# Filling two half-arrays by a count of time: the beats of a fused PixArt block

## The chip, the core and the metric

The kernel runs on one core of a Trainium2 chip. The metric is device time in microseconds (us) of one execution of the whole program; smaller is better. Beside the times of the runs there is one profiled execution, taken by the hardware profiler, from which all rows in this document come. Engines are named as in the profile: PE is TensorE's matmuls, PEld its weight loads, DVE is VectorE, ACT is ScalarE, POOL is GpSimd, SP is SyncE, which issues most DMAs.

## The reference

One transformer block with 16 batch rows of 256 tokens, 256 features, 16 heads of 16. Layout changes left out:

```python
shift_a, scale_a, gate_a, shift_m, scale_m, gate_m = jnp.split(silu(c) @ W_mod + b_mod, 6, axis=-1)
x_norm = modulate(_ln(x), shift_a, scale_a)
q, k, v = jnp.split(x_norm @ W_qkv + b_qkv, 3, axis=-1)
attn_w = softmax(einsum('bhqd,bhkd->bhqk', q, k) * scale)
x = x + gate_a[:, None] * (einsum('bhqk,bhkd->bhqd', attn_w, v) @ W_proj + b_proj)
q_c = _ln(x) @ W_qc + b_qc
k_c, v_c = jnp.split(_ln(context) @ W_kvc + b_kvc, 2, axis=-1)
c_attn_w = softmax(einsum('bhqd,bhsd->bhqs', q_c, k_c) * scale)
x = x + einsum('bhqs,bhsd->bhqd', c_attn_w, v_c) @ W_cproj + b_cproj
h = gelu(modulate(_ln(x), shift_m, scale_m) @ W_mlp1 + b_mlp1)
x = x + gate_m[:, None] * (h @ W_mlp2 + b_mlp2)
```

So each batch row has a self-attention, then a cross-attention over 256 context tokens, then a feed-forward part.

## The kernel before

The work of one attention of one batch row is a *unit*. There are 32: self-attentions of rows 0 to 3 first (units 0 to 3), then alternately a self-attention and, four rows behind, a cross-attention (`seq`, line 748); from unit 4 to 27 an even number is a self-attention (tiles named `_s`) and an odd one a cross-attention (`_c`). The last four units are cross-attentions, and the feed-forward part of all rows follows.

The main loop has one *step* for each unit, of eight *beats* (`beat(n, k)`, line 1025). Every engine's instructions keep the order in which the program writes them, so the order within `beat` is the order of every queue; only semaphores between engines and the filling of queues are left to the machine.

Each beat starts with `visit` (line 1006): four score matmuls `s` of the next unit, whose row maxima VectorE takes (`mx`, one reduction over both banks of the tile `s`), and four transposed score matmuls `st` of the present unit, of which ScalarE takes the exponential (`pt`). There is one `s` tile and one `st` tile of two banks each, so the next beat's `s` waits for this beat's maximum, and the next beat's `st` for this beat's exponential. Beats 0 and 4 then multiply the probabilities with V (`o`, 32 matmuls, emptied by ScalarE as `oT`). The other beats hold *lane work*.

Lane work uses one half of the array's rows at a time: partitions 0 to 63 are one row tile (lane 0), partitions 64 to 127 the other (lane 1), and instructions for both can be in flight together. A projection (K, Q, V or the output projection P) with its three products of split numbers is 12 matmuls of 64 rows by 256 columns on each half, `lane(o, half)` at line 418: first eight of the high parts, then four of the low part. Lane 0 opens the PSUM bank and lane 1 adds to it, some beats later; a `PE.nop()` that waits (`after`, line 314) stands ahead of the second half. Transposes too come in halves (`half_turns`, line 320): four instructions a half for a tile of 256 by 256, one a half for the maxima. `beside(a, b)` (line 454) takes one instruction from lane 0's list and one from lane 1's in turn; `take(it, n)` (line 449) is n instructions of a projection that goes on later.

In step n the lane work is, with u+2 and u+3 the units two and three ahead: beat 1, Q of u+2 beside P of u-2 and the second half of this unit's maxima; beats 2 and 3, transposes T of the normalised input of u+3 and A of the attention output of u-1, V of u+2 in lane 0, Q of u+2 in lane 1; beat 5, maxima of the next unit (`psm`, sent on as `m`), transposes aT of u-1's normalised output, K of u+3 in lane 0, V of u+2 in lane 1; beat 6, transposes T[1] (the cross-attention's query side, when u+3 is one: `lx`, which holds in even steps) and A of this unit, K of u+3 in lane 1; beat 7, P of u-1 in lane 0.

A transposed tile goes from PSUM through ScalarE (`evac`, tile `y`) to GpSimd, which splits it (`cut`, tiles `xTh` and `xTl`). `keep` (line 528) is ScalarE's copy of V out of PSUM. PSUM beside `s` and `st` has two rings of two banks: LONG for projections, SHORT for transposes, maxima and `o`; a bank is free when its last reader is done. In odd steps from 5 to 23 beat 6 is `light` (line 1054): its `s` goes to one bank of the tile and one of the SHORT ring, with a reduction for each.

Of the kernel before, what the change touches and what calls it, by code (L numbers as in the profile page):

```python
# [3 lines left out]

# [17 lines left out]
def pixart_block(  # L22
# [45 lines left out]
    def ps_gen(name, tag=None):  # L68


        if tag is None and ps_turn[0] is not None:
            ps_turn[0] ^= 1
            tag = (SHORT, LONG)[ps_turn[0]]
        tag = tag or SHORT
        return psum.tile([P, 512], F32, tag=tag, name=name, bufs=2)
# [234 lines left out]
    def whole(pieces, o):  # L310
        for i, p in enumerate(pieces):
            PE.transpose(o.ps[:, i * P:(i + 1) * P], p, ident)

    def after(name):

        gate = PE.nop()
        tc.add_manual_dep(gate.ins, name, mybir.DependencyInfo(
            mybir.DependencyClass.Sync, mybir.DependencyReason.DATA), reason="one bank, two halves of the array")

    def half_turns(pieces, o):  # L320


        done = []

        def half(h):
            rows = slice(64 * h, 64 * h + 64)
            for i, p in enumerate(pieces):
                if i == 0 and done:
                    after(done[0])
                ins = PE.transpose(o.ps[:, i * P + 64 * h:i * P + 64 * h + 64], p[rows], ident[rows, rows])  # L330
                if i == len(pieces) - 1:
                    done.append(ins.ins.name)
                yield
        return half(0), half(1)

    def transposed(src, name, scale=None, pool=False):
# [81 lines left out]
    def lane(o, half):  # L418


        rows = slice(half * 64, half * 64 + 64)
        if half:
            after(o.seen)
        for low in (False, True):
            for f in range(2):
                for k in range(KC):
                    for a, b in (((1, 0),) if low else ((0, 0), (0, 1))):
                        xT, W = o.src.xT, o.W
                        x_, w_ = xT[a][rows, k], W[b][rows, k]
                        if o.tok:  # L430
                            x_ = x_[:, f * P:(f + 1) * P]
                        else:
                            w_ = w_[:, f * P:(f + 1) * P]
                        ins = PE.matmul(o.ps[:, f * N:(f + 1) * N], *((x_, w_) if o.tok else (w_, x_)),
                                        start=o.fresh, stop=(half == 1 and low and k == KC - 1),
                                        skip_group_check=True)
                        o.seen = ins.ins.name
                        o.fresh = False
                        yield

    def lane0(x):
        if x:
            x.ps, x.fresh = ps_gen(f"ps_{x.name}", LONG), True
        return lane(x, 0) if x else iter(())

    def lane1(y):
        return lane(y, 1) if y else iter(())

    def take(it, n):
        for _ in range(n):  # L450
            next(it, None)
            yield

    def beside(a, b):
        for _ in zip_longest(chain(*a), chain(*b)):
            pass

    def to_stack(W, src, bias, dst, which, name):

# [301 lines left out]
    nu = len(units)  # L761
# [258 lines left out]
        later.append(lambda: exp(units[n], k, bank))  # L1020

    none = (), ()
    rest_x = rest_y = ()

    def beat(n, k):
        nonlocal rest_x, rest_y
        if n < 0:
            visit(n, k, (st, sp)[k % 2])
            return
        cur, prev, nxt = unit(n), unit(n - 1), unit(n + 1)  # L1030
        q2, q3, q4 = (v if v and v.n >= m else None
                      for v, m in zip(map(unit, (n + 2, n + 3, n + 4)), (1, 2, 3)))
        p1, p2, p3 = (v and v.post for v in map(unit, (n - 1, n - 2, n - 3)))
        apart = n > nu - 4
        if n - 2 > nu - 5:
            p2 = None
        if n - 3 > nu - 5 or p3 and p3.hurry:
            p3 = None
        lc = q4 if q4 and q4.kind == "c" else None
        ls = q4 if q4 and q4.kind == "s" else None  # L1040
        lx = q3 if q3 and q3.kind == "c" else None
        late = lx and lx.b in (0, 1, B - 2, B - 1)
        early = lc if lc and lc.b not in (0, 1, B - 2, B - 1) else None
        if k == 0 and q2:
            q2.K.high()
            q2.K.send_high()
        if k == 2 and p2:
            p2.end()
        if k == 4 and q2:
            q2.Q.high()  # L1050
            q2.Q.send_high()
        if k == 6 and q2:
            q2.V.keep()
        light = k == 6 and nxt and 3 < n < nu - 4 and not lx
        home = sp
        if light:
            home = sp[:, 0], ps_gen("s1", SHORT)
        elif nxt and n * 8 + k >= nu * 8 - 17 and k % 2:
            home = ps_gen("s0", LONG), ps_gen("s1", LONG)
        visit(n, k, home)  # L1060
        exps()
        if k == 0:
            if prev:
                av_part(prev, 2)
                av_part(prev, 3)
            if q2:
                q2.K.low()
                q2.K.send_low()
            if p3:
                p3.add()  # L1070
            if ls and n > 0:
                load(ls)
            if lc:
                lc.ln[0].steps[0]()
            if p1:
                p1.gate()
        elif k == 1:
            m = m_halves(cur, 1) if cur else none
            x, y = lane0(q2 and q2.Q), lane1(p2)
            beside([m[0], x], [take(y, 4), m[1], y])  # L1080
            if cur:
                m_send(cur, 1)
            if lc:
                lc.ln[0].steps[1]()
                lc.ln[0].steps[2]()
        elif k == 2:
            T = q3.T[0].halves() if q3 else none
            A = p1.halves(1) if prev else none
            x, y = lane0(q2 and q2.V), lane1(q2 and q2.Q)
            beside([T[0], A[0], take(x, 2)], [take(y, 10)])  # L1090
            rest_x, rest_y = [x], [T[1], A[1], y]
            if p2 and p2.hurry:
                p2.add()
        elif k == 3:
            beside(rest_x, rest_y)
            if q3:
                q3.T[0].evac()
                q3.T[0].cut()
            if prev:
                p1.norm(1)  # L1100
        elif k == 4:
            if cur:
                av_part(cur, 0)
                av_part(cur, 1)
            if q2:
                q2.Q.low()
                q2.Q.send_low()
            if p3:
                p3.store()
            if late:  # L1110
                for f in lx.ln[1].steps:
                    f()
            if ls and not late:
                ls.ln[0].steps[0]()
                ls.ln[0].steps[1](False)
        elif k == 5:
            m = m_halves(nxt, 0) if nxt else none
            aT = p1.aT.halves() if prev else none
            x, y = lane0(q3 and q3.K), lane1(q2 and q2.V)
            beside([m[0], take(x, 7), aT[0], x], [take(y, 2), aT[1], m[1], y])  # L1120
            if nxt:
                m_send(nxt, 0)
            if prev:
                p1.aT.evac()
                p1.aT.cut()
            if ls and late:
                for f in ls.ln[0].steps:
                    f()
            elif ls:
                ls.ln[0].pow()  # L1130
                ls.ln[0].steps[2]()
            if early:
                early.ln[1].steps[0]()
            v = unit(n + 5)
            if v and v.kind == "c":
                load(v)
        elif k == 6:
            if cur:
                cur.post.begin()
            T = lx.T[1].halves() if lx else none  # L1140
            A = cur.post.halves(0) if cur else none
            y = lane1(q3 and q3.K)
            beside([T[0], A[0]], [take(y, 8 if lx else 4)])
            rest_y = [T[1], A[1], y]
            if early:
                early.ln[1].steps[1]()
                early.ln[1].steps[2]()
            if prev and apart:
                p1.proj(0)
                p1.proj(1)  # L1150
        elif k == 7:
            beside([lane0(None if apart else p1)], rest_y)
            if lx:
                lx.T[1].evac()
                lx.T[1].cut()
            if prev and apart:
                p1.end()
                p1.add()
                p1.store()
            if cur:  # L1160
                cur.post.norm(0)
# [97 lines left out]
```

## Time and profile before

| | |
|---|---|
| median of 3 runs (lowest to highest) | 798.84 us (797.94 to 800.02) |
| the profiled execution's own time | 799.69 us |
| its span, first to last instruction | 797.9 us |
| mean granted TensorE clock | 0.999 |
| busy: PE / DVE / ACT / POOL | 97% / 74% / 70% / 66% |
| TensorE matmul instructions | 10066 |
| bytes moved by DMA | 87.96 MB, mean 110 GB/s |

The span is what the engines' instructions cover; the execution's own time is 1.8 us longer. Most instructions are issued through one helper, so their line is L51 and groups are told apart by the tiles they write and read. In a row of the timeline the columns are start, duration, engine, line, operation, output<-input, shape and count; in brackets stands the idle time before it and what ended it. In a row of stretches the columns are the stretch, its length, the busy time of PE, PEld, DVE, ACT and POOL with counts, the granted clock, the DMA share and GB/s. The chain of waits is followed back from the last instruction of a stretch; its rows give start, duration and what was worked on. In a row of a group the numbers behind the bar are busy us, mean ns of one, and idle us before them.

### The profile page before, as it was taken

How to read it: one execution, taken by the hardware profiler on the slowest of the kernel's cores; microseconds unless marked ns; L12 is line 12 of the kernel's file. 1: busy time of each engine (PE TensorE's matmuls, PEld its weight loads, DVE VectorE, ACT ScalarE, POOL GpSimd, SP SyncE). 2: the span in 40 equal slices, each digit the busy share in tenths (PEclk: the TensorE clock that was granted, in tenths of full speed). 3: DMA queues.
4: the chain of work that ended last, by engine and by line, in shares of the span. 5: the costliest groups of instructions: out<-in, count | busy, mean ns of one | idle time of the engine just before them, and what ended most of it. 6: DMA issues, size and time to landing. Idle time of an engine off the chain costs nothing.

```text
span 797.9 us, 25010 instructions
## 1 busy us (share of the span) xinstructions
PE 771.4 (97%) x10066; PEld 668.6 (84%) x10066; DVE 589.5 (74%) x1037; ACT 557.1 (70%) x961; POOL 529.4 (66%) x497
## 2 busy tenths in 40 slices
PE   8999999999999999999999999999899999999997
PEld 8778777888887887888888888877679999999997
DVE  5877878787788788888888888876674656656662
ACT  4267777787787877877777778776556666666663
POOL 6757849595775859567495878774546656666653
PEclk9999999999999999999999999999999999999999
DMA  6654444435344544534444554534311321211312
GB/s 206 146 152 130 109 120 123 109 107 154 104 133 108 148 122 108 161 97 128 122 127 141 138 146 121 159 100 120 95 43 42 93 61 60 81 59 62 81 41 53
DMA packets 89942, 87.96 MB, mean 110 GB/s; under 512 B 9506, under 2 KB 85572, under 8 KB 89828
## 3 DMA queue, kind: packets, MB, share of 16 engines
q1 hardware_dynamic: 89364, 85.58, 38.6%
q8 instruction: 80, 1.31, 0.7%
q0 software_dynamic: 192, 0.52, 0.3%
q14 instruction: 34, 0.28, 0.1%
q10 hardware_dynamic: 272, 0.26, 0.1%
HBM read 26.97 MB, written 8.46 MB: 44 GB/s over the span
## 4 chain that ended last, share of the span: by engine, by line
PE 60%; DVE 15%; POOL 9%; ACT 8%; issue 4%; DMA 2%; SPq 1%; POOLq 0%; ACTq 0%
PE o L51 14%; PE s L51 10%; PE st L51 7%; DVE mx L51 6%; DVE xn_m L51 4%; PE ps_qc L51 3%; PE ps_q L51 3%; POOL hl L51 3%; PE ps_v_c L51 3%; PE ps_P_s L51 3%; PE ph L51 3%; PE ps_k L51 2%; PE ps_v_s L51 2%; PE ps_kc L51 2%; PE ps_P_c L51 2%
## 5 line engine op out<-in xcount | busy, mean ns | idle before, releaser
L51 DVE TENSOR_REDUCE mx<-s 128x4 f32<-128x1024 f32 (+1 forms) x267 | 308.9, 1162 | 99.5 <-PE s L51 95.5
L51 ACT ACTIVATE pt<-st 128x1024 f32<-128x1024 f32 x252 | 259.5, 1030 | 79.8 <-PE st L51 68.2
L51 PE MATMUL s<-big 63*128 63x256 f32 (+1 forms) x1024 | 132.7, 315 | 4.1 <-DVE mx L51 1.8
L51 POOL TENSOR_TENSOR hl<-hf,hh 128x512 fp32r<-128x512 f32 x64 | 89.1, 1402 | 54.4 <-ACT hh L51 54.2
L51 PE MATMUL o<-pt,v 128*32 128x256 f32 x2048 | 123.8, 382 | 1.3 <-DVE A_c L51 0.4
L51 PEld LDWEIGHTS s<-big 63*128 63x128 f32 (+1 forms) x1024 | 86.5, 185 | 44.6 <-DVE mx L51 10.7
L51 PE MATMUL st<-big 64*128 64x256 f32 (+1 forms) x1024 | 116.2, 285 | 6.7 <-ACT pt L51 4.1
L51 PEld LDWEIGHTS st<-big 64*128 64x128 f32 (+1 forms) x1024 | 89.0, 186 | 12.2 <-ACT pt L51 6.7
L51 PEld LDWEIGHTS o<-pt,v 128*32 128x32 f32 x2048 | 60.4, 109 | 43.4 <-ACT y_s L51 3.1
L51 ACT ACTIVATE hf<-ph,bT 128x256 f32<-128x256 f32 x120 | 50.4, 474 | 27.5 <-PE ph L51 27.4
L51 ACT ACTIVATE hh<-ph,bT 128x256 fp32r<-128x256 f32 x120 | 50.5, 473 | 22.7 <-PE s L51 8.3
L51 ACT COPY oT<-o 128x512 f32<-128x512 f32 x63 | 37.0, 587 | 36.9 <-PE o L51 36.9
L51 PE MATMUL ph<-wqch,wself 128*128 128x256 f32 x256 | 51.4, 284 | 0.0
L51 PE MATMUL ph<-wkch,wself 128*128 128x256 f32 x256 | 51.4, 285 | 0.0
L51 POOL CAST xTh_c<-y_c 128x512 fp32r<-128x512 f32 x16 | 10.0, 626 | 56.5 <-ACT y_c L51 51.0
L51 PE MATMUL s<-big,hh 128*128 128x256 f32 x256 | 46.7, 281 | 0.0
L51 PE MATMUL st<-big,hh 128*128 128x256 f32 x256 | 46.5, 281 | 0.0
L51 DVE TENSOR_SCALAR xn_m<-x,mv_m,rs_m 128x256 f32<-128x256 f32 x32 | 38.2, 1234 | 10.8 <-POOL rs_m L51 10.8
L51 PEld LDWEIGHTS ph<-wqch,wself 128*128 128x128 f32 x256 | 41.5, 189 | 0.4 <-issue 0.4
L51 PEld LDWEIGHTS ph<-wkch,wself 128*128 128x128 f32 x256 | 41.5, 189 | 0.2
L51 PE MATMUL ps_k<-xTh_s,wself 64*128 64x256 f32 (+1 forms) x232 | 41.5, 293 | 0.0
L51 PE MATMUL ps_v_s<-wself,xTh_s 64*128 64x256 f32 x224 | 41.5, 295 | 0.0
(226 smaller groups left out, 2513.1 us busy)
## 6 DMA issues: line engine op xcount, KB each, us to landing
big<-h_kc SPq DMA_DIRECT2D x64, 128.0 KB
big<-h_qc SPq DMA_DIRECT2D x64, 128.0 KB
big<-h_k SPq DMA_DIRECT2D x62, 128.0 KB
big<-h_q SPq DMA_DIRECT2D x62, 128.0 KB
big<-l_k SPq DMA_DIRECT2D x32, 128.0 KB
big<-l_q SPq DMA_DIRECT2D x32, 128.0 KB
c<-in_ctx_dram SPq DMA_DIRECT2D x16, 256.0 KB
g<-gd SPq DMA_DIRECT2D x16, 256.0 KB
```

Source lines behind the costliest of these rows:

```text
L51: i = f(*a, **k)
```

## The change

Four edits, all in the order of lane work:

1. `beside` no longer takes turns. Each instruction yields its length, 1 for a projection matmul and `HALF = 0.53` for a half transpose, and the next instruction comes from the lane whose sum is smaller.
2. Lane work is spread differently over beats 2, 3, 5, 6 and 7. T and A are done within beat 2, the one half of A ahead of the other and opposite T; V takes 5 matmuls of lane 0 there and 7 in beat 3. Beat 5 holds 7 of K's and 7 of V's 12 matmuls and their last 5 move to beat 6, with the transposes of that beat in both lanes; K's second half is all in beat 7 beside P.
3. What hangs on these: T's `evac` and `cut` come at the end of beat 2 and no longer of beat 3; V's `keep` at the end of beat 6 and no longer at its start; `m_send` behind aT's `evac` and `cut`.
4. The `light` beat is gone: `s` of beat 6 always uses its own tile.

```diff
+    HALF = 0.53
...
@@ half_turns
-                yield
+                yield HALF
@@ lane
-                        yield
+                        yield 1
...
     def take(it, n):
         for _ in range(n):
-            next(it, None)
-            yield
+            yield next(it, 1)
 
     def beside(a, b):
-        for _ in zip_longest(chain(*a), chain(*b)):
-            pass
+        ab, at = [chain(*a), chain(*b)], [0, 0]
+        while min(at) < 1e9:
+            i = at[1] < at[0]
+            at[i] += next(ab[i], 1e9)
...
@@ beat
-        if k == 6 and q2:
-            q2.V.keep()
-        light = k == 6 and nxt and 3 < n < nu - 4 and not lx
         home = sp
-        if light:
-            home = sp[:, 0], ps_gen("s1", SHORT)
...
@@ k == 2
-            beside([T[0], A[0], take(x, 2)], [take(y, 10)])
-            rest_x, rest_y = [x], [T[1], A[1], y]
+            beside([T[0], take(x, 5), A[0]], [A[1], take(y, 5), T[1]])
+            rest_x, rest_y = x, y
+            if q3:
+                q3.T[0].evac()
+                q3.T[0].cut()
@@ k == 3
-            beside(rest_x, rest_y)
-            if q3:
-                q3.T[0].evac()
-                q3.T[0].cut()
             if prev:
                 p1.norm(1)
+            beside([rest_x], [rest_y])
@@ k == 5
-            beside([m[0], take(x, 7), aT[0], x], [take(y, 2), aT[1], m[1], y])
-            if nxt:
-                m_send(nxt, 0)
+            beside([m[0], take(x, 4), aT[0], take(x, 3)], [aT[1], take(y, 1), m[1], take(y, 6)])
+            rest_x, rest_y = x, y
             if prev:
                 p1.aT.evac()
                 p1.aT.cut()
+            if nxt:
+                m_send(nxt, 0)
@@ k == 6
-            y = lane1(q3 and q3.K)
-            beside([T[0], A[0]], [take(y, 8 if lx else 4)])
-            rest_y = [T[1], A[1], y]
+            beside([A[0], take(rest_x, 5), T[0]], [T[1], take(rest_y, 5), A[1]])
+            if q2:
+                q2.V.keep()
@@ k == 7
-            beside([lane0(None if apart else p1)], rest_y)
+            beside([lane0(None if apart else p1)], [lane1(q3 and q3.K)])
```

More of the change, by code (lines that the diff above doesn't have):

```diff
@@ L1 @@
 from collections import defaultdict
-from itertools import chain, zip_longest
+from itertools import chain
 from contextlib import ExitStack
@@ L1022, in pixart_block @@
     none = (), ()
-    rest_x = rest_y = ()
+    rest_x = rest_y = iter(())
     def beat(n, k):
@@ L1051, in beat @@
             q2.Q.send_high()
-        if k == 6 and q2:
-            q2.V.keep()
-        light = k == 6 and nxt and 3 < n < nu - 4 and not lx
         home = sp
-        if light:
-            home = sp[:, 0], ps_gen("s1", SHORT)
-        elif nxt and n * 8 + k >= nu * 8 - 17 and k % 2:
+        if nxt and n * 8 + k >= nu * 8 - 17 and k % 2:
             home = ps_gen("s0", LONG), ps_gen("s1", LONG)
```

## The prediction

> **What bounds the kernel now.** I read the page first, for the busiest engine, then one stretch of 100 us from the middle, then the timeline of a single step of the loop beat by beat, engine by engine, and last the chain of waits for the beats that are longer than their work.
>
> ```profile
> PE 771.4 (97%) x10066; PEld 668.6 (84%) x10066; DVE 589.5 (74%) x1037; ACT 557.1 (70%) x961; POOL 529.4 (66%) x497
> ```
>
> ```profile
> 300.00:400.00 100.00, 98.77 (x1540) 82.53 (x1531) 82.62 (x141) 78.83 (x122) 68.25 (x67) 1.00 0.46 124
> ```
>
> TensorE counts as busy 98.8% of a middle stretch at the full granted clock (1.00), but a busy TensorE may have one half of its array empty, and the mean hides which beats it limits. The start of each beat's `s` matmuls shows the beats. Step 15 (current unit a cross-attention, "odd") runs from 298.78 to 315.80; step 16 ("even") follows.
>
> ```profile
> 298.78 0.48 PE L51 MATMUL s<-big 63*128 63x256 f32 x4
> 301.29 0.50 PE L51 MATMUL s<-big 63*128 63x256 f32 x4
> 303.39 0.43 PE L51 MATMUL s<-big 63*128 63x256 f32 x4
> 305.14 0.50 PE L51 MATMUL s<-big 63*128 63x256 f32 x4
> 306.96 0.50 PE L51 MATMUL s<-big 63*128 63x256 f32 x4
> 309.65 0.51 PE L51 MATMUL s<-big 63*128 63x256 f32 x4
> 312.10 0.28 PE L51 MATMUL s<-big 63*128 63x256 f32 x1
> ...
> 313.40 0.51 PE L51 MATMUL s<-big 63*128 63x256 f32 x4
> 315.80 0.47 PE L51 MATMUL s<-big 63*128 63x256 f32 x4
> ...
> 323.96 0.51 PE L51 MATMUL s<-big 63*128 63x256 f32 x4
> 326.49 0.50 PE L51 MATMUL s<-big 63*128 63x256 f32 x4
> 328.94 0.28 PE L51 MATMUL s<-big 63*128 63x256 f32 x1
> ...
> 330.89 0.50 PE L51 MATMUL s<-big 63*128 63x256 f32 x4
> 332.82 0.47 PE L51 MATMUL s<-big 63*128 63x256 f32 x4
> ```
>
> Differences give beats 0 to 7 of the odd step: 2.51, 2.10, 1.75, 1.82, 2.69, 2.45, 1.30, 2.40 (17.02 us). Of the even step, beats 4 to 7: 2.53, 2.45, 1.95, 1.93.
>
> Inside a beat the halves work at their own rates:
>
> ```profile
> 303.87 0.22 PE L51 MATMUL psT_s<-ident,xn_s 64*128 64x64 f32 x1
> 303.90 0.28 PE L51 MATMUL ps_qc<-xTh_q,wqch 64*128 64x256 f32 x1
> ...
> 304.30 0.23 PE L51 MATMUL psA_s<-ident,oT 64*128 64x64 f32 x1
> 304.37 0.28 PE L51 MATMUL ps_qc<-xTh_q,wqch 64*128 64x256 f32 x1
> ```
>
> The first and last of eight transposes start 0.43 apart, 0.061 each; the first and fifth projection matmul start 0.47 apart, 0.117 each (one "slot"). In the program's order the eighth transpose stands behind the seventh of these matmuls, yet it starts before the fifth. So TensorE's queue already lets the quicker half run ahead: a beat costs about the longer half's own time, not the count of pairs.
>
> Beats that end before TensorE's work would allow are held by VectorE, whose maximum must be out of the `s` banks before the next beat's `s`:
>
> ```profile
> 303.86 1.22 DVE L51 TENSOR_REDUCE mx<-s 128x4 f32<-128x1024 f32 x1
> ...
> 305.68 1.22 DVE L51 TENSOR_REDUCE mx<-s 128x4 f32<-128x1024 f32 x1 [0.60 <-PE s L51]
> ```
>
> ```profile
> 326.43 0.74 DVE L51 BATCH_NORM_STATS2 st_s<-x 128x6 f32<-128x256 f32 x2
> 327.09 0.30 DVE L51 BATCH_NORM_AGGREGATE mv_s<-st_s 128x2 f32<-128x6 f32 x2
> ...
> 327.50 1.22 DVE L51 TENSOR_REDUCE mx<-s 128x4 f32<-128x1024 f32 x1
> 329.61 1.22 DVE L51 TENSOR_REDUCE mx<-s 128x4 f32<-128x1024 f32 x1 [0.89 <-PE s L51]
> ```
>
> Beat 2: the maximum starts 0.47 after `s`, ends at 305.08, and `s` follows at 305.14. Beat 3: 0.54, ends 306.90, `s` at 306.96. Even beat 6: 0.67 (a half still had backlog), ends 330.83, `s` at 330.89. So there is a floor: 1.75, 1.82 and 1.95 for the three.
>
> **The change part by part.**
>
> *Filling by time, beats 2 and 3.* Lane work of beat 2 was the longer half's 10 slots, now 4 + 4 transposes at 0.53 and 5 slots, 9.24; beat 3 falls from 10 slots to 7. Both sit on the floor of 1.75 and 1.82, so I put the gain at zero; bounds: 0 and -0.08 (beat 3 at beat 2's floor).
>
> *Beat 5.* Before: 0.53 + 7 + 2.12 + 5 = 14.65 slots a half. Now 0.53 + 4 + 2.12 + 3 = 9.65. The five slots go to beat 6: 5 x 0.117 = 0.58, so 2.45 becomes 1.87. In the odd step VectorE permits it (0.54 + 1.22 + 0.06 = 1.82, as in beat 3). In the even step it doesn't: its beat 4 also holds LayerNorm statistics, its maximum starts only 1.01 after `s` (327.50 against 326.49) and ends at 328.72; with 0.06 the next `s` is at +2.29. So the even beat 5 gains only 2.45 - 2.29 = 0.16.
>
> *Beat 4, odd.* The transposed tile is now evacuated at the end of beat 2, ahead of the beat-3 exponential on ScalarE. The chain shows what the old place cost:
>
> ```profile
> 306.92 0.82 ACT y_s L51 x2
> 307.74 0.04 issue
> 307.79 1.93 PE o L51 x32
> ```
>
> `o` takes the bank that `y_s` empties and waited for it. The even step, with one 0.58 evacuation, shows the beat without that wait: 2.53. Gain 2.69 - 2.53 = 0.16. The evacuation now goes ahead of exponential 3: it ends some 0.1 + 0.82 after beat 2's lane work (1.63, below), at 2.55, and that exponential could not start before 1.75 + 0.85 = 2.60 anyhow (0.85 is beat 5's, next fence). Its cut stands in POOL's queue behind the same work as before.
>
> *Beats 6 and 7, and V one step on.* ScalarE's order changes:
>
> ```profile
> 310.50 1.03 ACT L51 ACTIVATE pt<-st 128x1024 f32<-128x1024 f32 x1
> 311.42 0.25 ACT L51 ACTIVATE m<-psm 16x128 fp32r<-16x128 f32 x1
> 311.87 0.59 ACT L51 COPY y_as<-psT_as 128x512 f32<-128x512 f32 x1 [0.20 <-PE psT_as L51]
> 312.53 0.59 ACT L51 COPY v<-ps_v_c 128x512 f32<-128x512 f32 x1
> 313.01 1.03 ACT L51 ACTIVATE pt<-st 128x1024 f32<-128x1024 f32 x1
> ```
>
> Now: exponential 5, `y`, `m`, exponential 6, `v`, exponential 7. Counted from beat 5's `s`: exponential at 0.85 (310.50 - 309.65), `y` 0.92 later at 1.77, `m` at 2.25 (0.48 after a copy, as 312.53 to 313.01), done 2.50. In beat 6 the first transposes need the banks of `y` (2.36) and, being the second bank in the ring, of `m` (2.50); in the odd step TensorE comes there at 1.87 + 0.48 = 2.35 (0.48 as in beat 2) and waits 0.15, with everything behind it in its one queue. Lane work of odd beat 6 is 7.12 slots, 0.83, done by 3.4: the floor is later. Maximum 6 starts when the statistics let it (1.76 + 0.66, the step from 326.43 to 327.09, is 2.42; `s` + 0.54 is 2.41), ends 3.64, and `s` 7 is at 3.70. Exponential 6 starts at 1.87 + 0.85 = 2.72, `v` 0.92 later, done 4.23; the output projection, which takes V's bank, comes there at 3.70 + 0.48 to 0.61 (beats 2 and 5): at most 0.05 of wait. Beat 7 has 12 slots as the even one has, 1.93. So odd beats 6 and 7: 1.83 + 1.93 = 3.76, against 3.70 with the split maximum that is dropped: a loss of 0.06. Even: `s` 6 at 2.29 comes after `m`; the maximum 0.54 later ends 4.05, `s` 7 at 4.11, beat 6 is 1.82 and not 1.95, because both halves of beat 5 now end together: gain 0.13; beat 7 unchanged.
>
> *Queues moved past.* `m` goes behind `y` on ScalarE; its two DMAs follow on SP:
>
> ```profile
> 312.06 1.43 SPq L51 DMA_DIRECT2D big<-m  x2
> ```
>
> They are issued by 2.41 + 1.43 = 3.84 after beat 5's `s`, now 2.50 + 1.43 = 3.93, and first read 0.3 into the next step, at 5.95 instead of 6.45: 2.0 us of slack for landing instead of 2.6. POOL's cut could become the next late thing:
>
> ```profile
> 295.32 0.61 POOL L51 CAST xTh_ac<-y_ac 128x512 fp32r<-128x512 f32 x1 [2.76 <-PE ps_v_s L51]
> ...
> 309.49 0.61 POOL L51 CAST xTh_s<-y_s 128x512 fp32r<-128x512 f32 x1
> ```
>
> ```profile
> 310.26 0.36 PE L51 MATMUL ps_k<-xTh_s,wself 64*128 64x256 f32 x1
> ```
>
> From the first cut of an even step POOL works without a gap to 310.10, 14.78 us; K in odd beat 5 needs that. The cut will start at 2.42 in even beat 5, so it ends at 17.20; K wants it at 16.7 + 0.61 = 17.3. Slack 0.1; without it K waits at most some 0.3 us in each odd step.
>
> *The price that no row has.* Transpose against transpose, one in each half, does not occur before; now it does, eight pairs in beat 2 and eight in an even beat 6. Lower bound 0.061 a pair (each half at its own rate). Upper, far: two weight loads in a row, 0.28:
>
> ```profile
> L51 PEld LDWEIGHTS psT_s<-ident,xn_s 64*128 64x128 f32 (+1 forms) x116 | 10.9, 139 | 1.0 <-POOL xn_s L51 0.9
> ```
>
> Eight transposes and four matmuls with their loads start in 303.87 to 304.30, 0.036 an instruction, hence 0.072 a pair; this is nearest in kind and I take it. Beat 2 is then 0.47 + 8 x 0.072 + 0.58 = 1.63, under the floor.
>
> *Sum.* Ten odd steps (5 to 23): -0.58 - 0.16 + 0.06 = -0.68 each, -6.8. Eleven even steps (6 to 26): -0.16 - 0.13 = -0.29, -3.2. Steps 1 and 3 have no split maximum: -0.74 each, -1.5; step 25 likewise without the beat-4 part, -0.6. Steps 0, 2, 4 and from 27 on I leave at zero, some because their beat 6 waits for a late normalisation that comes no sooner. Together -12.1. The profiled execution of 799.69 becomes 787.6 (its span 797.9 becomes 785.8); it stands 0.85 above the median of the runs shown, 798.84, so the forecast on that scale is 786.7.
>
> **Rivals.** *Slower: transposes in both halves get in each other's way.* Place: beat 2 of some 27 steps and beat 6 of eleven. The cost over the floors is 27 x (8p - 0.69) + 11 x (8p - 0.77) = 304p - 27; it eats the 12.1 us at p = 0.128 a pair, about one after the other (2 x 0.061 = 0.122). At the 0.139 of one full load a pair it is +15.2, and the time 802. For it: loads are long (139 ns) and never seen side by side as a pair; against it: 0.036 an instruction above. The Trainium skill's page "TensorE: Matmul & The Clock Gate", section "LDWEIGHTS (loading the stationary operand)", gives a load as its columns over 1.2 ns, 107 ns for 128; were the two loads strictly one after the other, a pair would take an estimated 213 ns and the time come out near 824. By that rule, three loads per 0.117 us in beat 2 would not fit; the trace has them.
>
> *The gain is mostly given back to the floors.* If the maximum starts 0.67 after `s` as in even beat 6, and not 0.5, beats 2, 3, 5 and 6 rise by 0.1 to 0.2, together some 0.35 a step over 24 steps, 8.4 us: 795. For it: VectorE and ScalarE are at 83% and 79% of a middle stretch already. The skill's "TensorEngine Tiling (Array Packing)", section "PSUM Bottleneck", says the same in general: tiling speeds up TensorE and not the emptying of its banks. The trace agrees, with the floor of 1.75 to 1.95 under 1.22 us of maximum.
>
> *More than forecast.* Beats 3 and 6 fall to 1.75 as well, 2 x 0.08 over 24 steps, -3.8: 783.
>
> *The count of time does nothing,* since the queue runs ahead anyhow: true of beats 2 and 3, and in the sum as zero; beat 5 is different, since work leaves it.
>
> **How the numbers follow.** Forecast 786.7: chance 0.57, by itself 783.5 to 791 (POOL's 0.3 in ten steps, the bounds of beat 3). Floors, 795 (791 to 799): 0.20. More, 783 (780 to 784): 0.10. Slower, 802 and up: 0.13. A measurement here tells 0.3%, 2.4 us. Faster takes the forecast, the third and two thirds of the second: 0.80; same 0.07; slower 0.13. The range leaves out the slower case and the tails: 780 to 798.
>
> **What will show it.** Odd beat 5 at 1.9 and even beat 5 at 2.3; odd beat 6 at 1.85, with a single maximum, odd beat 7 at 1.9; odd beat 4 at 2.53 with no `y_s` ahead of `o`; beats 2 and 3 unchanged. Steps of 16.4 (odd) and 16.7 (even). Wrong if beat 2 grows past 1.8 (pairs), if TensorE waits for `v`, `m` or POOL's `xTh_s` by more than 0.3, or if maxima start later than 0.55 after `s`.

## The result and the profile after

The changed kernel takes 801.57 us (median of 20 runs, 798.84 to 806.3), the kernel before 799.15 (20 runs beside them, 797.47 to 800.04): ratio 1.0034, 95% interval 1.0020 to 1.0049. It is slower by a third of a per cent where 1.5% faster was forecast. Its profiled execution took 800.28 us with a span of 798.2, one of its quicker ones. Of all runs told below one is left out of medians and ratios, the first of g4_mix: it took 894.72 us at a mean granted clock of 0.753.

The busy line of the page of the changed kernel, and the middle stretch in the columns of the one shown before (PE, PEld, DVE, ACT, POOL, clock, DMA share, GB/s):

```profile
PE 766.0 (96%) x10066; PEld 656.9 (82%) x10066; DVE 589.3 (74%) x1027; ACT 562.0 (70%) x961; POOL 528.4 (66%) x497
```

```profile
300.00:400.00 100.00, 98.13 (x1558) 80.89 (x1552) 83.93 (x139) 80.39 (x123) 69.28 (x69) 1.00 0.45 125
```

Ten reductions fewer (1027 against 1037: the light beats), and in the middle 1558 matmuls in 100 us, not 1540: there the kernel is 1.2% quicker. The `s` rows of the timeline of the changed kernel, the end of step 14, step 15 (odd) and step 16 (even):

```profile
298.68 0.42 PE L51 MATMUL s<-big 63*128 63x256 f32 x4
301.13 0.50 PE L51 MATMUL s<-big 63*128 63x256 f32 x4
303.24 0.43 PE L51 MATMUL s<-big 63*128 63x256 f32 x4
305.01 0.48 PE L51 MATMUL s<-big 63*128 63x256 f32 x4
306.82 0.50 PE L51 MATMUL s<-big 63*128 63x256 f32 x4 [0.25 <-DVE mx L51]
309.41 0.50 PE L51 MATMUL s<-big 63*128 63x256 f32 x4
311.53 0.41 PE L51 MATMUL s<-big 63*128 63x256 f32 x4
313.27 0.50 PE L51 MATMUL s<-big 63*128 63x256 f32 x4
315.38 0.45 PE L51 MATMUL s<-big 63*128 63x256 f32 x4
...
323.66 0.50 PE L51 MATMUL s<-big 63*128 63x256 f32 x4 [0.25 <-DVE mx L51]
326.19 0.51 PE L51 MATMUL s<-big 63*128 63x256 f32 x4
328.47 0.50 PE L51 MATMUL s<-big 63*128 63x256 f32 x4
330.30 0.51 PE L51 MATMUL s<-big 63*128 63x256 f32 x4
332.42 0.42 PE L51 MATMUL s<-big 63*128 63x256 f32 x4
```

The odd step has beats of 2.45, 2.11, 1.77, 1.81, 2.59, 2.12, 1.74, 2.11 (16.70, forecast 16.4, before 17.02). The even step's beats 4 to 7 are 2.53, 2.28, 1.83, 2.12; with its first half it takes 17.04, as long as before (17.02), forecast 16.7.

Step for step, from the starts of each step's first `s` in the two profiled executions (after less before): steps 0, 1 and 3 together -2.3; steps 5 to 26 -6.3; **step 2 +4.0; steps 4, 27 and 28 +0.6, +0.6 and +1.5; from step 30 on +2.1**. The steps that the forecast costed (1, 3 and 5 to 26) gave 7.6 of its 12.1; those it left at zero took all of that back.

Part of the 6.3 is not the change. In some even steps beat 4 lasts longer than 2.53: in step 24 of the kernel before it takes 3.62, and its `st` matmuls wait 0.70 in it for `m`, which a DMA brings. Over the eleven even steps the excess is 4.0 us in the profile before and 2.6 in the one after; in the other profiles it lies between 1.1 and 3.1, in no order that follows the edits.

**Step 2.** The timeline of the kernel before, POOL and VectorE; `t_s` and the `x` behind it are the gated residual sum of the self-attention (`add`), `xTh_c` and `xTl_c` the cut of T[0]:

```profile
77.91 1.29 POOL L51 TENSOR_TENSOR t_s<-t_s,g 128x512 f32<-128x512 f32 x1 [2.75 <-ACT t_s L51]
79.28 1.29 POOL L51 TENSOR_TENSOR x<-xg,t_s 128x512 f32<-128x512 f32 x1
81.15 0.61 POOL L51 CAST xTh_c<-y_c 128x512 fp32r<-128x512 f32 x1 [0.59 <-ACT y_c L51]
...
83.03 0.74 DVE L51 BATCH_NORM_STATS2 st_q<-x 128x6 f32<-128x256 f32 x2
```

And of the changed kernel, with TensorE's first transpose of the second half of T[1]:

```profile
78.38 0.61 POOL L51 CAST xTh_c<-y_c 128x512 fp32r<-128x512 f32 x1 [4.55 <-ACT y_c L51]
79.07 1.28 POOL L51 TENSOR_TENSOR xTl_c<-y_c,xTh_c 128x512 fp32r<-128x512 f32 x1
80.31 1.29 POOL L51 TENSOR_TENSOR t_s<-t_s,g 128x512 f32<-128x512 f32 x1
81.68 1.27 POOL L51 TENSOR_TENSOR x<-xg,t_s 128x512 f32<-128x512 f32 x1
...
82.99 0.75 DVE L51 BATCH_NORM_STATS2 st_q<-x 128x6 f32<-128x256 f32 x2 [1.19 <-POOL x L51]
...
85.34 0.50 PE L51 MATMUL s<-big 63*128 63x256 f32 x4 [1.29 <-DVE mx L51]
...
87.54 0.37 PE L51 MATMUL psT_q<-ident,xn_q 64*128 64x64 f32 x1 [0.86 <-POOL xn_q L51]
```

In steps 2 and 28 (whose unit u-2 belongs to the first or last batch row, `hurry`) `p2.add()` stands in beat 2 too. T's evacuation and cut moved to the end of beat 2 came to stand ahead of it. On POOL the cut now waits 4.55 us for its input with the sum queued behind it. So `x` comes 1.93 us later in POOL's queue (78.38 to 80.31, the cut's two operations) and behind the cut's own wait: it is done 11.9 us after the start of the step, and 8.2 in the kernel before. VectorE waits 1.19 us for it with this beat's maximum behind, TensorE waits 1.29 for the maximum, and then 0.86 for `xn_q` with everything behind it in its one queue.

Then something comes that no row of before shows. The stretches from the second wait on, of the changed kernel and of the kernel before (same columns; the clock is the third number from the right):

```profile
86.39:93.21 6.82, 5.96 (x60) 5.78 (x62) 2.92 (x4) 2.84 (x4) 6.60 (x7) 0.50 0.23 77
```

```profile
86.39:93.21 6.82, 5.99 (x95) 4.56 (x96) 5.32 (x10) 4.50 (x8) 6.63 (x7) 1.00 0.51 140
```

After these idles the granted clock is at half for 6.83 us, and TensorE is busy as long for 60 matmul rows as for 95 before. Over the changed kernel's runs the mean granted clock goes from 0.989 (806.3 us) to 0.998 (799.6): the correlation of time and clock is -0.78 over 20 runs. Its times spread over 7.5 us, where the kernel before has 2.6 in the 20 runs beside them (but 4.6 to 6.2 in the later rounds).

### The profile page after: what moved, and what is told of

The parts are those of the page before. It is cut to its first block, busy times and chain, and to the rows that moved or that the text cites. A ratio compares the mean times of both kernels' runs of the same rounds, so it can differ in the third digit from the quotient of the medians.

```text
span 798.2 us, 24978 instructions
## 1 busy us (share of the span) xinstructions
PE 766.0 (96%) x10066; PEld 656.9 (82%) x10066; DVE 589.3 (74%) x1027; ACT 562.0 (70%) x961; POOL 528.4 (66%) x497
## 4 chain that ended last, share of the span: by engine, by line
PE 63%; DVE 15%; POOL 9%; issue 5%; ACT 5%; DMA 2%; SPq 1%; POOLq 0%; ACTq 0%; DVEq 0%
PE o L51 14%; PE s L51 12%; PE st L51 7%; DVE mx L51 7%; DVE xn_m L51 4%; PE ps_P_s L51 3%; PE ps_P_c L51 3%; PE ps_v_c L51 3%; POOL hl L51 3%; PE ph L51 3%; PE ps_v_s L51 2%; POOL x L51 2%; PE ps_kc L51 2%; PE ps_q L51 2%; PE ps_qc L51 2%
## 5 line engine op out<-in xcount | busy, mean ns | idle before, releaser
L51 PE MATMUL s<-big 63*128 63x256 f32 (+1 forms) x1024 | 123.8, 314 | 12.0 <-DVE mx L51 10.9
L51 PEld LDWEIGHTS s<-big 63*128 63x128 f32 (+1 forms) x1024 | 81.1, 187 | 50.0 <-DVE mx L51 22.3
L51 PE MATMUL st<-big 64*128 64x256 f32 (+1 forms) x1024 | 110.1, 284 | 4.7 <-ACT pt L51 3.1
L51 PEld LDWEIGHTS st<-big 64*128 64x128 f32 (+1 forms) x1024 | 83.4, 187 | 8.2 <-ACT pt L51 3.7
L51 POOL CAST xTh_ac<-y_ac 128x512 fp32r<-128x512 f32 x15 | 9.2, 614 | 54.5 <-ACT y_ac L51 54.5
```

What stands on the lines that cost most here:

```text
L51: i = f(*a, **k)
```

## The experiments

The kernel before, run beside them, took 799.78 us beside the experiments whose names begin with e, 799.57 beside f1 to f4, and 797.99 beside f5 and g1 to g4; h1_mix has one run of 800.31 beside it. Ratios are to these. "The changed kernel" is 801.57, and where two experiments are compared by their times, they were not always run side by side. Lengths of beats and steps are from the one profiled execution of each.

**The order of the hurry steps** (e1_hurry), the changed kernel with the sum back ahead of the cut:

```diff
@@ k == 2
+            if p2 and p2.hurry:
+                p2.add()
             if q3:
                 q3.T[0].evac()
                 q3.T[0].cut()
-            if p2 and p2.hurry:
-                p2.add()
```

> The changed kernel with one order restored: in beat 2 of steps 2 and 28 the residual addition of two units back goes to GpSimd ahead of the cut of the transposed tile. Theory W (the loss sits in a few steps whose beat 6 waits for a late normalisation): the addition ends 1.9 us sooner in the queue, the late normalised tile of step 2 comes about 1.2 us sooner, TensorE's idle time there falls under what lets the clock drop, and step 2 goes from 21.8 to 17.5 to 18.5 us, step 28 from 21.5 to about 20.5; the median falls by 3 to 6 us, to about 797, and the granted clock rises to 0.997 or more. Theory S (the loss is spread over all steps by bank waits): less than 1 us of change.

Measured: 796.38 (12 runs), ratio 0.9967 [0.9952, 0.9983]; 5.2 us less than the changed kernel, for two operations that change places. In its timeline of POOL and VectorE in step 2:

```profile
78.08 1.29 POOL L51 TENSOR_TENSOR x<-xg,t_s 128x512 f32<-128x512 f32 x1
79.31 0.60 POOL L51 CAST xTh_c<-y_c 128x512 fp32r<-128x512 f32 x1
...
81.87 0.74 DVE L51 BATCH_NORM_STATS2 st_q<-x 128x6 f32<-128x256 f32 x2
```

VectorE no longer waits, no stretch of half clock is left but the one behind the last work, and step 2 takes 18.46 instead of 21.86: beat 5 1.28 less (the wait for the maximum), beats 6 and 7 2.06 less. The waits for `xn_q` within these two are as long in both (0.20 and 0.93 here, 0.20 and 0.86 in the changed kernel), so the 2.06 are the clock. Step 28 takes 20.2 instead of 21.5. So this order is the largest single loss, shown.

**The clock by itself** (e3_warm), the changed kernel with idle matmuls (into a bank that nobody reads) in beat 5 of the four late steps. `d6` issues twelve of them, so each step has 24 and not the twelve that the expectation names:

```diff
-(30, 0): 'd3', ...
+(2, 5): 'd6 d6', (4, 5): 'd6 d6', (27, 5): 'd6 d6', (28, 5): 'd6 d6', (30, 0): 'd3', ...
```

> The changed kernel with twelve idle matmuls on zeros between beats 5 and 6 of steps 2, 4, 27 and 28, where TensorE otherwise waits; the waits stay. If the dropped clock is a cost of its own: step 2 falls from 21.8 to about 18.5 us at a full clock, the granted clock of the runs is 0.998 to 0.999 instead of 0.989 to 0.998, their times spread over 2 us instead of 7, and the median falls by 2 to 4 us. If the clock only goes along with the waits and costs nothing by itself: no change, or 0.5 us more for the extra matmuls.

Measured: 803.97 (6 runs), 1.0051 [1.0032, 1.0070], slower than the changed kernel. The clock was 0.998 or more in every run and the scatter fell to 4 us, but the idle matmuls cost more than they saved. Their row in step 4:

```profile
121.56 2.94 PE L51 MATMUL ps_warm<-wz 128*128 128x128 f32 x24 [0.38 <-ACT y_as L51]
```

They take 2.94 us and first wait 0.38 for a bank. Step 4, which has no half clock in the changed kernel's profile, takes 9.48 for beats 5 to 7, against 7.81. Step 2 takes 9.48, against 11.16: with the clock held, it is no worse than step 4. What the clock costs is thus not told apart here from what the fillers cost; the 2.06 above are the better figure.

**V ahead of aT in beat 5** (e4_vfirst):

```diff
@@ k == 5
-[aT[1], take(y, 1), m[1], take(y, 6)]
+[take(y, 2), aT[1], m[1], take(y, 5)]
```

> The changed kernel with lane 1 of beat 5 beginning with two of V's matmuls and the transposes behind them. Theory B (the first transpose waits 0.2 us for the bank that ScalarE empties of the attention output): beat 5 of odd steps goes from 2.11 to about 1.9, of even steps it stays between 2.1 and 2.3, bound by VectorE; in all 2 to 3 us less. Rival (0.2 us is what a half loses each time it turns from transposes to projection matmuls): beat 5 stays at 2.1 and the time within 1 us.

Measured: 801.1 (12 runs), 1.0020 [1.0004, 1.0037]: no gain over the changed kernel. It was meant to take away this, seen in the timeline of the changed kernel in odd beat 5:

```profile
309.55 0.58 ACT L51 COPY oT<-o 128x512 f32<-128x512 f32 x1 [0.81 <-PE o L51]
...
310.19 0.27 PE L51 MATMUL psT_as<-ident,A_s 64*128 64x64 f32 x1
...
310.29 0.36 PE L51 MATMUL ps_k<-xTh_s,wself 64*128 64x256 f32 x1
...
310.49 0.28 PE L51 MATMUL ps_k<-xTh_s,wself 64*128 64x256 f32 x1
```

The first aT takes the SHORT bank that `o` leaves, starts only when `oT`'s copy (to 310.13) is done, and K stands behind it. K's second matmul then follows 0.20 after the first and not 0.117: a turn from transposes to projections costs 0.08. With V ahead, that wait is gone, but lane 0's aT now waits 0.07 for lane 1's, which opens the bank, and odd beat 5 takes 2.09, as long.

**The count of time alone** (e5_fill), on the kernel before: `HALF`, the yields and the new `beside`, with every list as it was.

> The kernel before with its lists of lane work as they were, and only the count of time in place of taking turns. By the prediction the queue runs ahead anyhow, so the beats stay as they were and the time within 1.5 us of before. Rival: the order by time is itself worth something or costs something, and beats 2, 3, 5 or 6 change by 0.1 us or more, 3 us in all.

Measured: 794.85 (5 runs), 0.9939 [0.9917, 0.9960]. The forecast's "does nothing" is refuted. In its timeline, even beat 6 of step 16, after the same place of the kernel before, where V's half still works beside the first `s`:

```profile
328.94 0.28 PE L51 MATMUL ps_v_s<-wself,xTl_s 64*128 64x256 f32 x1
...
329.18 0.28 PE L51 MATMUL s<-big 63*128 63x256 f32 x1
```

```profile
325.05 0.42 PE L51 MATMUL s<-big 63*128 63x256 f32 x4
325.51 1.23 DVE L51 TENSOR_REDUCE mx<-s 128x4 f32<-128x1024 f32 x1 [0.62 <-PE s L51]
326.79 0.50 PE L51 MATMUL s<-big 63*128 63x256 f32 x4
```

The beat is 1.74, not 1.95: the maximum starts 0.46 after `s`, not 0.67, since the two halves of beat 5 end together and no backlog of one half delays the second pair of `s` (from 329.18 on before, 0.24 after the first). Odd beats 6 and 7 go from 1.30 and 2.40 to 1.19 and 2.26 to 2.29, beat 5 of even steps from 2.45 to 2.39.

**And its reverse** (g2_nofill), the changed kernel with `HALF = 1`, so that the lanes take turns again.

> The changed kernel with the count of time taken out: a transpose counts as a whole slot again, so that the two halves are dealt out one by one, with all new lists kept. The forecast held that the count of time does nothing: then it takes 800 to 803, as the changed kernel does. If the fill is what makes the halves end together, transposes of one half stand against projections of the other, its beats 2, 3, 5, 6 come out 0.05 to 0.3 longer, and it takes 805 to 812.

Measured: 805.53 (4 runs), 1.0087 [1.0059, 1.0114]: 4.0 above the changed kernel. Odd beats 5 to 7 are 2.24, 1.89, 2.11 instead of 2.12, 1.74, 2.11. Both ways round the count of time is worth 4 to 5 us.

The four kernels with and without each part can be compared in the middle, steps 5 to 26, away from the rare steps and without even beat 4 (medians of the profiled executions):

| | odd step | even step less beat 4 | together |
|---|---|---|---|
| kernel before | 17.04 | 14.50 | 31.54 |
| count of time alone (e5_fill) | 16.85 | 14.26 | 31.11 |
| new lists alone (g2_nofill) | 16.98 | 14.59 | 31.57 |
| both (changed kernel) | 16.69 | 14.46 | 31.15 |

In the middle the gain is the count of time, 0.43 for two steps or 4.7 us over eleven pairs. The new lists give nothing there, with it or without: what they gain in the odd step (0.16 and 0.06) they lose in the even one (0.20 and 0.09). All other kernels with the count of time, but f2_vwhole, lie between 31.13 and 31.21.

**T behind all other lane work in the late steps** (f1_tlast), on top of e1_hurry:

```diff
@@ k == 6
+            if late:
+                beside([A[0], take(rest_x, 5), T[0]], [take(rest_y, 5), A[1]])
+                beside([], [T[1]])
+            else:
                 beside([A[0], take(rest_x, 5), T[0]], [T[1], take(rest_y, 5), A[1]])
```

> The run before it with the addition first (796.4 us), and beside that, in beat 6 of steps 2, 4, 27 and 28 alone, the two halves of the late transpose at the end of the lane work and no longer at its head. Theory W (what costs there is that ten projection matmuls moved from beat 5 stand behind the transpose that waits): beats 5 to 7 of those steps go from 7.8 to about 7.2 us, as in the kernel before, 2 to 2.5 us in all, median about 794. Rival (the step ends when GpSimd's normalised tile comes, whatever stands behind): no change within 0.5 us, or slower, since the transpose's two halves now run one after the other.

Measured: 795.39 (10 runs), 0.9946 [0.9924, 0.9969]; not to be told from e1_hurry by the times, but steps 2, 4 and 27 take 17.7 each instead of 18.5 and step 28 19.6 instead of 20.2, 3.0 together. Its timeline in step 2:

```profile
86.05 0.73 PE L51 MATMUL psT_q<-ident,xn_q 64*128 64x64 f32 x4 [0.53 <-POOL xn_q L51]
```

The wait is 0.53, and it comes when all other work of the beat is done.

**V whole in beat 5** (f2_vwhole), on top of e1_hurry: all V of lane 1 in beat 5, `keep` at the start of beat 6, as before the change.

> The changed kernel with the addition first, and V's second half again whole in beat 5 with its copy at the start of beat 6, as in the kernel before; K's split over beats 5 and 6 stays. If beat 7 is 2.1 to 2.3 us because the output projection waits for V's copy: beat 7 falls to 1.9 to 1.95 in all steps, beat 5 rises to about 2.5 and beat 6 to between 1.8 and 2.1, because the copy stands ahead of the exponential. If beat 7 is long because K's second half now fills lane 1 there: beat 7 stays at 2.1 or more.

One run: 804.95, odd beats 5 to 7 2.25, 2.19, 2.00, together 0.47 more. But it shows what beat 7 costs without V's copy. First the changed kernel at the head of beat 7 of step 18, then f2_vwhole in step 15:

```profile
364.37 0.36 PE L51 MATMUL s<-big 63*128 63x256 f32 x1
...
364.41 0.58 ACT L51 COPY v<-ps_v_s 128x512 f32<-128x512 f32 x1
...
365.14 0.36 PE L51 MATMUL ps_P_c<-wcph,xTh_ac 64*128 64x256 f32 x1
...
365.34 0.28 PE L51 MATMUL ps_P_c<-wcpl,xTh_ac 64*128 64x256 f32 x1
```

```profile
316.47 0.51 PE L51 MATMUL s<-big 63*128 63x256 f32 x4 [0.46 <-DVE mx L51]
...
317.05 0.28 PE L51 MATMUL ps_P_s<-wself,xTh_as 64*128 64x256 f32 x1
...
317.17 0.39 PE L51 MATMUL ps_P_s<-wself,xTh_as 64*128 64x256 f32 x2
```

P comes 0.77 after `s` when V's copy (to 364.99) is late, and its second matmul 0.20 after its first; with V gone early, 0.58 and 0.12, and the beat takes 2.00 instead of 2.11 to 2.30.

**K's first seven ahead of aT** (f3_order5), on top of e1_hurry, so that K fills the wait for `oT`'s bank:

```diff
@@ k == 5
-[m[0], take(x, 4), aT[0], take(x, 3)], [aT[1], take(y, 1), m[1], take(y, 6)]
+[m[0], take(x, 7), aT[0]], [take(y, 2), aT[1], m[1], take(y, 5)]
```

> The changed kernel with the addition first, and beat 5's lane 0 as maxima, seven of K's matmuls, transposes, lane 1 as two of V's, transposes, maxima, five of V's. With the first transposes later they don't wait for the bank of the attention output (0.2 us), and with the other half's three matmuls later than that its gate finds them done (0.23 us where they followed at once). Odd beat 5 goes from 2.11 to 1.85 to 1.95, 2 to 2.5 us in all, median about 794; even steps gain nothing, VectorE bounds them. Rival: a half pays 0.08 us at each turn from transposes to projections and that is what is left: odd beat 5 stays above 2.05.

Measured: 800.58 (10 runs), 1.0015 [0.9993, 1.0037], 4.2 above e1_hurry. Odd beats 5 and 6 do fall to 1.83 and 1.83 (the floor), beat 7 rises to 2.23, the odd step takes 16.62 instead of 16.70. But steps 2 and 27 take 1.2 longer each, with the clock at half for 3.41 us in both. Of step 2:

```profile
84.50:87.89 3.39, 1.92 (x30) 1.44 (x28) 2.69 (x7) 1.94 (x4) 3.20 (x5) 1.00 0.45 121
87.89:91.30 3.41, 3.41 (x40) 3.41 (x38) 1.68 (x3) 1.81 (x3) 3.31 (x4) 0.50 0.52 154
```

In the 3.4 us before, TensorE's gaps add up to 1.47 (3.39 less 1.92). The waits for `xn_q` in them are as in e1_hurry, 0.20 and 0.93; new is 0.34 ahead of them, where beat 6's `s` waits for the maximum, because beat 5's lane work is done sooner and VectorE is not. Step 27 has the same three waits.

**The tail's halves in two beats** (f4_tail), on top of e1_hurry: where there are no projections to put between them, the two halves of A in two beats as before the change (beats 2 and 3 of steps 30 and 31, beats 6 and 7 from step 29 on).

> The changed kernel with the addition first, and in steps 30 and 31 (beats 2 and 3) and from step 29 on (beats 6 and 7) the two halves of the attention output's transposes in two beats, as in the kernel before, where there is no projection to lie between them. If the loss at the end (from the start of step 30, 2.0 us) is the gate of the second half waiting for the first, some 0.3 us in each of six places: the end falls by 1.5 to 2 us, median about 794.5. Rival (the end is set by the feed-forward part's own chain): within 0.5 us.

Measured: 796.74 (10 runs), 0.9961 [0.9942, 0.9981], the same as e1_hurry by the times. In the profiled executions beats 1 to 6 of step 30 fall from 14.97 to 13.93, and all from the start of that step to the end from 238.2 to 236.6 (236.1 in the kernel before). The transposes of its beat 2, in e1_hurry and in f4_tail:

```profile
564.59 0.92 PE L51 MATMUL psA_c<-ident,oT 64*128 64x64 f32 x8
```

```profile
564.03 0.40 PE L51 MATMUL psA_c<-ident,oT 64*128 64x64 f32 x4
```

With nothing to put between, the second half stands behind the first and its gate, and the beat grows by 0.5 (beats 2 and 6 of the step).

**Together** (g1_best: e1_hurry, f1_tlast and f4_tail; f5_all: with f3_order5 too).

> The changed kernel with three edits together, each tried alone before: the addition of the hurry steps ahead of the transposes' copy and cut, T of the late steps behind everything else in beat 6, and the tail's halves in two beats as before. If the three gains lie in different steps they add: the hurry order gave about -5, T last gave -0.8 in each of steps 2, 4 and 27 and -0.6 in step 28, the tail -1.05 in step 30, so 796.4 - 3.0 - 1.0 = 792.4 (ratio 0.991 to 0.993). The rival is that the late steps and the tail only shift waits to work that the last store follows anyway: then it stays at 795 to 796.

> As g1_best, with K's first seven ahead of aT in beat 5 (that order alone came out at 800.6, not faster than 796.4 without it, though its odd steps were 16.62 and not 16.69: steps 2 and 27 took 1.2 longer each, with TensorE waiting for xn_q and its clock at half for 3.41 us). With T last those waits are gone: if they alone ate the order's gain, this one is faster than g1_best by 0.5 to 1.5, about 791.5. If it is slower than g1_best by over 1, the order costs something outside steps 2 and 27.

Measured: 792.80 (6 runs), 0.9921 [0.9899, 0.9944], and 792.48 (4 runs), 0.9919 [0.9895, 0.9944]. Both are faster than both kernels. Steps 2, 4 and 27 take 17.7, step 28 19.6, beats 1 to 6 of step 30 13.9, with no half clock before the end. The order of beat 5 adds nothing that can be told: what odd beats 5 to 7 gain (5.88 for 5.96) goes back in the next step's beat 0 (2.60 for 2.50).

**The new beats 5 to 7 in the odd steps alone** (g4_mix, and h1_mix, the same kernel for its profile), on top of e5_fill.

> The kernel before with the count of time alone, and the new beats 5 to 7 only in the odd steps in the middle, with K's first seven ahead of aT there (K fills the 0.2 us in which aT waits for oT's bank). If the count of time is the gain and the spread is worth something only where both halves had a short and a long beat (odd steps 16.85 in the first, 16.62 with that order), eleven odd steps bring 0.2 to 0.25 each: 792 to 793, the fastest of all. If the spread of beats 5 to 7 gives nothing in itself, it stays at 794 to 796.

> The same kernel as g4_mix again, for its profile alone. If the new odd steps run as in f3_order5 (16.62, against 16.85 with the count of time alone), the gain must be lost in the even steps behind them or at the seams, where old and new lists meet: even beats 5 to 7 over 2.39, 1.75, 1.93, or odd beat 0 over 2.5. If the odd steps themselves are 16.8 or more, the order of the new beats needs the other parity's lists too.

Measured: 795.56 (11 runs), 0.9965 [0.9951, 0.9978], and one run of 795.6 for h1_mix: not faster than the count of time alone. The profile of h1_mix shows odd beats 5 to 7 at 1.83, 1.83, 2.23 (5.88, against 5.97 in e5_fill), and the next beat 0 at 2.60 instead of 2.53: most of the tenth is lost at the seam. Its odd beat 4 is 2.69, as the lists of beats 2 and 3 are the old ones.

## Why the prediction was wrong

*Right.* Even beat 6 at 1.79 to 1.83 (forecast 1.82), beat 3 on its floor (1.80 to 1.83), odd beat 6 under 1.83 with a single maximum, odd beat 4 near its mark (2.59 for 2.53). Even beat 5 is at 2.28 (forecast 2.29, the maximum behind the statistics) in three of the eleven even steps and at 2.12 in the others. The rival of later maxima is not borne out: in beats 2, 3 and 6 they start 0.45 to 0.53 after `s` (medians). The rival of pairs of transposes is refuted. The timeline of the changed kernel in beat 2 of step 16, which is 1.83 long, has them side by side:

```profile
320.62 0.22 PE L51 MATMUL psT_c<-ident,xn_c 64*128 64x64 f32 x1
320.63 0.22 PE L51 MATMUL psA_c<-ident,oT 64*128 64x64 f32 x1
320.68 0.22 PE L51 MATMUL psT_c<-ident,xn_c 64*128 64x64 f32 x1
320.69 0.22 PE L51 MATMUL psA_c<-ident,oT 64*128 64x64 f32 x1
320.95 0.38 PE L51 MATMUL ps_v_s<-wself,xTh_s 64*128 64x256 f32 x1
...
321.17 0.28 PE L51 MATMUL ps_v_s<-wself,xTh_s 64*128 64x256 f32 x1
```

That is 0.06 a pair, the lower bound; 0.072 was taken. The Trainium skill, "TensorE: Matmul & The Clock Gate", section "LDWEIGHTS (loading the stationary operand)", gives a load as its columns over 1.2 ns, an estimated 107 ns here; one after the other, as the prediction's rival had it, two would take an estimated 0.21 us, and the trace has 0.06. So the two row halves' loads run together.

What the sum of beat 2 (1.63) lacks is the turn: when both halves go from transposes to projections at once, the first projections come 0.26 later and the second 0.22 after them, where the rates are 0.06 and 0.12. That is 0.30 more, and pairs of 0.06 for 0.072 are 0.10 less, which makes 1.83 of 1.63. So beat 2 did grow past 1.8 in the even steps, one of the prediction's signs of being wrong, from 1.74 to 1.84 (odd steps 1.78), but for another reason than pairs.

Two things failed: steps that the sum left at zero, and the price of the moved work itself.

*"Steps 0, 2, 4 and from 27 on I leave at zero, some because their beat 6 waits for a late normalisation that comes no sooner."* It comes later, in two of them. The prediction followed the moved cut past the work ahead of it ("behind the same work as before") and not past the work behind it in the two steps that have `p2.add()` in the same beat. Undone, that is 5.2 us (e1_hurry), of which 4.7 can be read in the profiled executions (3.4 in step 2, 1.3 in step 28). Beside it, T at the head of lane 1 puts all lane work of the late steps behind `xn_q`, where before V and K stood ahead of it: 3.0 us (f1_tlast against e1_hurry in those four steps). And the tail's halves: 1.7 from the start of step 30 to the end, 1.0 of them in that step (f4_tail against e1_hurry, in the profiled executions alone). Nothing of the three is in the sum.

*"5 x 0.117 = 0.58, so 2.45 becomes 1.87"* (odd beat 5) measured 2.12. The price of the matmuls that leave was right; what was missed is what is late next, `oT`'s copy out of the bank that aT needs (0.2), hidden until then by K's first seven, and 0.08 for a turn from transposes to projections. With K ahead again it is 1.83 (f3_order5).

*"At most 0.05 of wait. Beat 7 has 12 slots as the even one has, 1.93"*, and the even beat 7 "unchanged": measured 2.11 in odd steps and 2.11 to 2.30 in even ones. Here two sizes are off. Twelve slots in both halves with no transposes among them cost 2.00 without any wait (f2_vwhole); the rest, 0.11 to 0.30, comes with V's copy behind exponential 6. Where even beat 5 is 2.12, beat 7 is 2.28 to 2.30; where it is 2.28, beat 7 is 2.12. Beats 5 to 7 of the even step so take 6.21, and 6.33 before: a gain of 0.12 and not 0.29. The count of time alone has 6.06 there.

*"The count of time does nothing, since the queue runs ahead anyhow"* was given as true of beats 2 and 3 and priced at zero. It is worth 4.9 us by itself, and in the middle it is the whole gain: two steps go from 31.54 to 31.11 with it alone. The moved lists, to which the sum gives all its 12.1, are worth nothing there (31.57 with them alone). The queue does let the quicker half run ahead, as shown, but at a beat's end the slower half is what `s` waits for. The sum even had the mechanism, as "because both halves of beat 5 now end together", and put it down to the lists.

So the account is: count of time -4.9 (e5_fill); the three losses outside the middle +5.2, +3.0 and +1.7; the new lists in the middle about nothing. Added, +5.0, against the +2.4 measured; the 2.6 between are about what the intervals allow (1.2 to 1.7 us either way for the runs of each kernel). By the times of whole runs, g1_best at 0.9921 and e5_fill at 0.9939 (measured at different times, and the intervals overlap), the new lists with the three losses mended may be worth 1.4 us more. Whether they are is open; it is not the 12 us of the forecast.

## What to carry to other kernels

When a block of calls moves in a written order, list for every queue what it has passed in either direction, in the rare steps (first, last, hurried) too: one swapped pair in two of 32 steps cost 5.2 us, about as much as the whole middle gained. A beat with slack on its busiest engine will show the next late thing, here a bank, a copy, a normalisation, so a saving is to be costed against the second-latest arrival and not against the work alone. And fill two parallel halves by time, not by count, before moving any work between them.

## What was not expected of the hardware

Short idles of TensorE were followed by half clock, and a grid in time decided which. The stretches of half clock last 3.41 us (once 6.83, two of them), and within a run they start a whole number of such lengths apart: in f3_order5 at 87.89 and 517.97, which is 126.0 of 3.413; in e4_vfirst at 87.13 and 537.69, 132.0; in the changed kernel at 86.39 and, behind the last work, at 796.36, 208.0. Laid on that grid in all profiles but that of g4_mix, 14 of them, between 40 and 560 us, the gaps between TensorE's rows added up to 1.44 us or more in eight windows, and behind seven of these half clock followed (the eighth, of 1.48 in the changed kernel, went without); in all other windows at full clock they added up to 1.41 or less, and none was followed by it. No single gap was longer than 1.3 us in step 2 of the changed kernel. Its first window at half clock had 0.86 of gaps and was followed by a second; the other six had 0.43 or less and were not. The Trainium skill, "TensorE: Matmul & The Clock Gate", in Part 1 on the clock gate, section "What's actually happening", describes a free-running window of 3413 ns, which agrees, and has the clock go down after an idle window; here 42% of a window idle was enough. If the grid's phase differs from run to run, so does what an idle of this size costs, which would explain much of the scatter; with one execution of each kernel profiled, that is argued and not shown. e1_hurry, for one, has 1.37 in one window, with no drop in its profile, and 0.995 to 1.000 as the mean clock of its runs.

A transpose of one half beside one of the other costs 0.06 us for the pair, no more than one alone (changed kernel, 320.62 to 320.68). A half that turns from transposes to projections loses 0.08 us once (310.29 to 310.49, where 0.12 is the rate); more when both turn together (0.26 and 0.22 in beat 2 of step 16).
